# A graph network in three edge stages: a new order of work in the head, in layer 1 and in the attention stage

## The chip, the cores and the metric

The kernel runs on one core of a Trainium2 chip. A core has a matrix engine (PE; its weight loads have a row of their own, PEld), a vector engine (DVE), a scalar engine (ACT), a general-purpose engine (POOL), which here issues the gathers, and SP, which issues plain transfers. Engines run side by side and wait for one another through semaphores. The metric is the device time of one execution in microseconds (us); lower is better.

## The reference, cut to what matters

The graph has N = 12500 nodes with D = 128 features and E = 400000 edges, sorted by target node. Two relational layers with R = 10 relations are followed by one attention layer with 4 heads of 32 features (GAT).

```python
def _rgcn_layer(x, src, dst, edge_type, w_rel, root, bias):
    seg = dst * NUM_REL + edge_type
    xs = x[src]
    sums = segment_sum(xs, seg); cnt = segment_sum(ones, seg)
    mean = (sums / maximum(cnt, 1)).reshape(N, NUM_REL, -1)
    return einsum('nrd,rdo->no', mean, w_rel) + x @ root + bias

# first block
edge_type = argmax(edge_attr_42[:, 16:26])
h = relu(layernorm(x))
x = x + _rgcn_layer(relu(_rgcn_layer(h, ..., w_rel1, root1, b1)), ..., w_rel2, root2, b2)
# second block (GAT)
h = relu(layernorm(x))
xl, xr = h @ W_l, h @ W_r                    # 4 heads x 32
score = einsum(leaky_relu(xr[dst] + xl[src], 0.2), att)
ex = exp(score - segment_max(score, dst)[dst])
out = segment_sum(ex / segment_sum(ex)[dst] * xl[src])
x = x + out + bias
```

## The kernel before, in words

The edges are cut into G = 125 groups of 128 x 25: a partition holds 25 edges that follow one another, and a group covers few enough target nodes that a 128-wide window of nodes holds them. The relational layers are turned round: a table of `h @ w_rel` for every node and relation is computed first, and each edge then gathers its row of 128 floats. So the program has four stages.

1. **Head** (`first_table`, to about 283 us): node tiles of 128 are normalised (`stats`, `norm`), transposed on PE (`turn`), put through a ReLU on ACT (`relu`) and multiplied with the ten matrices `wall`; the table goes to memory in 640 KB stores. A quad is four tiles and has one load of `x`. SP issues all 26 loads of `x` at the start, with the two edge lists `dst_i` and `src_i` as whole transfers between them. `analysis` is a generator whose steps run one per tile, from tile LEAD on.
2. **Layer 1** (`layer1`, to about 4890 us): the edge sums of the first layer, and from each finished 128-node window the table of the second layer.
3. **Layer 2** (`layer2`, to about 9320 us): the edge sums of the second layer, and the products `xl`, `xr` for GAT.
4. **GAT** (the code from L860, to 14040 us).

Stages 2 to 4 are loops with one turn per group. The order of the instructions within a turn is written by hand (`tc.manual_schedule()`): each engine runs its instructions in the order of the code, across groups at different depths. POOL issues in each turn 25 indirect gathers of one row per partition (L496 in the layers, L479 in GAT), as far ahead as there are free buffers: in layer 1 six half groups `xs`, in GAT five groups `xs`. A gather into a buffer waits for its last reader.

*A turn t of layer 1*, in this order: the gathers of group t and the loads; `node(t-2)`, which takes the PE sums `ps` of its group (carry add at L697), finds the carry `last` and makes `hT` with a ReLU on ACT (L706); `prepare(t+4)`, which finds relations and counts and sends their ends through PE (px, L624) to ACT (`ro`, L627); for group t-1 the `one_hots`, 24 `products` on ACT (L528, the second half of the edges, 13 + 12 edges to the halves and two products an edge) and `half_sums` on DVE (L516 and L519, the wide sum of the first half); `table(t-3)`, three matmuls (L714) with three copies on ACT (L716), one add on DVE (L718) and two stores by SP; `inflow(t+2)`, which begins with a copy of the carry `tr` on ACT (L650); `weights(t+1)`; `keep(t+5)` (ACT, L598); last the second half's reduction (L534) and `sums` (PE, L553) with the root matmul (L770). `ke` and `px` have one buffer each, `pt` and `ps` two.

*A turn t of GAT*: the gathers of t; two `z` copies by ACT (L931), each of up to 7 edges' target rows, from the PSUM tile `xn` (made by `prepare` in the turn before: PE multiplies one-hots `st` with the node rows `xr`, for the first and the last target of each half); `score(0)` to `score(3)`, each of them one copy_predicated (L937), an add with the gathered rows (L939), the leaky ReLU with `att` (L941) and a reduction (L943) on DVE; between them `inflow` and `end` and `add_up` of group t-3; then `maxima(t-1)` (two transposes on PE, L957, and the ACT copy `ro`, L960), `prepare(t)`, and ACT's copy `su` of the sums (`take`). `add_up` ends with `sums`: five pairs of a scaled block `xw` (DVE L1002, and a column copy by ACT, L1005) and a one-hot block `s` (DVE L1007), each pair feeding five matmuls (L1011). `xw` and `s` come from the pool `go`, four buffers each.

Of the kernel before, what the change touches and what calls it, by code (L numbers as in the profile page):

```python
# [18 lines left out]
P = 128  # L19
# [7 lines left out]
def kernel(  # L27
# [299 lines left out]
    def first_table():  # L327

        Q = 4
        LEAD = 12  # L330
        full = N // P
# [3 lines left out]
        tiles = [(q, k) for q, ts in enumerate(quads) for k in range(len(ts))]  # L335
        with tc.tile_pool(name="vw", bufs=1) as wp, tc.tile_pool(name="vx", bufs=1) as xp, \
                tc.tile_pool(name="vh", bufs=4) as hp, tc.tile_pool(name="vt", bufs=4) as tp, \
# [3 lines left out]
            wall = wp.tile([P, R * D], F32, name="wall")  # L341
            b2b = bcast_row(wp, b2, "b2b")
            dst_i = ap.tile([P, G, J], I32, name="dst_i")
            xs = []
            for q, ts in enumerate(quads):
                n = len(ts)
                r = starts[ts[0]]
                xq = xp.tile([P, Q, D], F32, name=f"xq{q}")
                nc.sync.dma_start(xq[:, :n, :], x[r:r + n * P, :].rearrange("(k p) d -> p k d", p=P))
                xs.append(xq)  # L350
                if q == 0:
                    nc.scalar.dma_start(wall.rearrange("d (r o) -> d r o", r=R), w_rel1.rearrange("r d o -> d r o"))
                if q == min(3, len(quads) - 1):
                    nc.sync.dma_start(dst_i, dstv)
                if q == min(6, len(quads) - 1):
                    nc.sync.dma_start(src_i, srcv)
            nc.sync.dma_start(hT_d[:, NP - P:], zero[:, :P])
            nc.sync.dma_start(xb_d[NP - P:, :], zero[:, :D])
            tv = t1_d.rearrange("(n r) d -> n (r d)", r=R)
# [47 lines left out]
            for i in range(3):  # L407
                norm(i)
            for i in range(2):
                turn(i)  # L410
                relu(i)
            look = analysis(ap, pp, dst_i)
            for i, (q, k) in enumerate(tiles):
                hT = hTs[q][:, k, :]
                ts = tp.tile([P, R * D], F32, name="ts")
# [26 lines left out]
                if k == n - 1:  # L442
                    r = starts[quads[q][0]]
                    xb = xp.tile([P, Q, D], F32, name=f"xb{q % 2}")
                    nc.vector.tensor_add(xb[:, :n, :], xs[q][:, :n, :], b2b[:, None, :].to_broadcast([P, n, D]))
                    nc.sync.dma_start(xb_d[r:r + n * P, :].rearrange("(k p) d -> p k d", p=P), xb[:, :n, :])
                    nc.sync.dma_start(hT_d[:, r:r + n * P], hTs.pop(q)[:, :n, :].rearrange("d k p -> d (k p)"))
            for _ in look:
                pass


    def sorted_edges():
# [4 lines left out]
        with tc.tile_pool(name="sd", bufs=1, space=DRAM) as sd, tc.tile_pool(name="sk", bufs=1) as sk:  # L457
# [29 lines left out]
            with tc.tile_pool(name="mid", bufs=1) as mid:  # L487
# [68 lines left out]
                def layer1():  # L556
                    with tc.tile_pool(name="fk", bufs=1) as kp, tc.tile_pool(name="fx", bufs=6) as xp, \
# [87 lines left out]

                        def inflow(g, rs, ps, before):

                            tr = wp.tile([R, P + 1], F32, name="tr")
                            if g:
                                nc.scalar.copy(tr[:, 0:1], before[:, P:])  # L650
                            else:
                                nc.vector.memset(tr[:, 0:1], 0.0)
                            nc.vector.tensor_tensor_scan(tr[:, 1:], ps[g][:, 0, :], rs[g][2][:, 0, :], tr[:, 0:1],
                                                         op0=OP.mult, op1=OP.add)
# [13 lines left out]
                            nc.scalar.copy(io, pc)  # L668
                            return io, tr

# [38 lines left out]
                        def table(g, hT, xb, b):  # L709
                            ts = wp.tile([P, (R + 1) * D], F32, name="ts")  # L710
                            for c in range(0, (R + 1) * D, 512):
                                n = min(512, (R + 1) * D - c)
                                pt = p3.tile([P, 512], F32, name="pt")
                                nc.tensor.matmul(pt[:, :n], hT, wall[:, c:c + n], start=True, stop=True)  # L714
                                m = min(n, R * D - c)
                                nc.scalar.copy(ts[:, c:c + m], pt[:, :m])  # L716
                                if m < n:
                                    nc.vector.tensor_add(ts[:, R * D:], pt[:, m:n], xb)  # L718
                            nc.sync.dma_start(t2v[ds(b, P), :], ts[:, :R * D])
                            nc.sync.dma_start(acc2_d[g], ts[:, R * D:])  # L720

# [4 lines left out]
                        with tc.manual_schedule():  # L726
                            for t in range(-4, G + 3):
# [10 lines left out]
                                if 0 <= q < G:  # L738
                                    nodes[q] = load_node(q)
                                q = t - 2  # L740
                                if 0 <= q < G:
                                    hTs[q], last = node(q, pss.pop(q), last)
                                q = t + 4
                                if 0 <= q < G:
                                    rs[q] = prepare(q, ms.pop(q), ke)
                                q = t - 1
                                if 0 <= q < G:
                                    ss = one_hots(sp, q)
                                    y1 = products(yp, by_slot(sp, q, 1), xs[q][1], 1)
                                    rr = [half_sums(yp, sp, by_slot(p2, q, 0), xs[q][0], 0)]  # L750
                                q = t - 3
                                if 0 <= q < G:
                                    table(q, hTs.pop(q), *nodes.pop(q)[1:])
                                q = t + 2
                                if 0 <= q < G:
                                    ios[q], tr = inflow(q, rs, ps, tr)
                                q = t + 1
                                if 0 <= q < G:
                                    weights(q, *rs[q][:2], keep(q), ios.pop(q))
                                    rs.pop(q), ps.pop(q)  # L760
# [3 lines left out]
                                if 0 <= q < G:  # L764
# [6 lines left out]
                                                     skip_group_check=True)  # L771
                                    xs.pop(q)

                def layer2():
# [86 lines left out]
            with tc.tile_pool(name="gk", bufs=1) as kp, tc.tile_pool(name="gx", bufs=5) as xp, \  # L861
                    tc.tile_pool(name="gw", bufs=2) as wp, tc.tile_pool(name="gs", bufs=3) as sp, \
                    tc.tile_pool(name="go", bufs=4) as op, \
                    tc.tile_pool(name="gc", bufs=4) as cp, tc.tile_pool(name="gn", bufs=6) as np_, \
# [5 lines left out]
                iotap = bank[:, :P]  # L870
                exps = [bank[:, k * P:k * P + H * J].rearrange("p (h j) -> p h j", h=H) for k in (1, 2)]
                nc.vector.tensor_copy(iotap, iota)
                att8 = kp.tile([P, D], F32, name="att8")
# [19 lines left out]
                def flat(t):  # L893
                    return t.rearrange("p h j -> p (h j)")
# [101 lines left out]
                def sums(g, xs, sc, po, before):  # L996
                    ex = exps[g % 2]
                    nc.scalar.activation(ex, sc, AF.Exp)
                    ex = ex.rearrange("p h j -> p j h")
                    for j0 in range(0, J, JW):  # L1000
                        xw = op.tile([P, JW, H, AW], F32, name="xw")
                        nc.vector.tensor_mul(  # L1002
                            xw[:, :, :, :C], xs[:, j0:j0 + JW, :D].rearrange("p j (h c) -> p j h c", h=H),
                            ex[:, j0:j0 + JW, :, None].to_broadcast([P, JW, H, C]))
                        nc.scalar.copy(xw[:, :, :, C], ex[:, j0:j0 + JW, :])  # L1005
                        s = op.tile([P, JW, P], F32, name="s")
                        nc.vector.tensor_tensor(s, iotap[:, None, :].to_broadcast([P, JW, P]),  # L1007
                                                dst_b[:, g, j0:j0 + JW, None].to_broadcast([P, JW, P]),
                                                op=OP.is_equal)
                        for j in range(JW):  # L1010
# [31 lines left out]
                with tc.manual_schedule():  # L1042
                    for t in range(G + 1):
# [485 lines left out]
```

## Time and profile before

| what | value |
|---|---|
| runs, median (lowest to highest) | 14032.24 us (14024.25 to 14067.41) |
| profiled execution | 14041.59 us |
| its span on the core | 14039.8 us |
| mean granted PE clock | 0.558 of full |
| DVE busy | 9212.9 us, 66% |
| POOL busy | 9120.0 us, 65% |
| PE and PEld busy | 3446.7 us and 2310.3 us |
| ACT busy | 2298.5 us |
| layer 1, 280 to 4890 us: DVE / POOL / ACT busy | 2838.0 / 2967.4 / 1365.6 us |
| GAT, 9560 to 14040 us: DVE / POOL / ACT busy | 3465.2 / 2829.2 / 689.5 us |

A group's row in the page names its line, engine and operation, the tiles written and read, the count, the busy time with the mean of one instruction in ns, and the engine's idle time just before such instructions with what ended it. "issue" is a wait for nothing that the profile shows, "remote" one for which no releaser was found. A line of the timeline gives start, duration, engine, line, operation, tiles and count, and in brackets the idle time before it with its releaser; an end of a matmul in it is modelled. The gathers' own busy time is the making of their descriptors, and a small issue time between two of them is not counted as busy.

### The profile page before, as it was taken

The numbers are of one execution on the slowest core, as the hardware profiler recorded it, in microseconds if no ns is written. First come the engines' busy times: TensorE is split into PE (matmuls) and PEld (weight loads), VectorE is DVE, ScalarE is ACT, GpSimd is POOL, SyncE is SP. The second block draws the span as 40 slices with busy tenths as digits, with TensorE's granted clock in tenths as the row PEclk, the third lists the DMA queues.
The fourth block names the chain that finished last, engine by engine and source line by source line (L and its number), as shares of the span: only waits on it lengthen the run. The fifth ranks groups of instructions, "written<-read, shape, count | busy, mean of one in ns | idle before, by whom it ended". The sixth has DMA issues, their size and how long they took to land.

```text
span 14039.8 us, 68433 instructions
## 1 busy us (share of the span) xinstructions
PE 3446.7 (25%) x12832; PEld 2310.3 (16%) x12832; DVE 9212.9 (66%) x12638; ACT 2298.5 (16%) x6975; POOL 9120.0 (65%) x9384
## 2 busy tenths in 40 slices
PE   6122222222222211111111111112333333333333
PEld 3011111111111100000000000002222222222223
DVE  7566666666666565555555565656777777777777
ACT  2233223333232200000000000001111111111111
POOL 1666666666666577777777666655666666666664
PEclk8555555555555555555555555555666666666666
DMA  8222222222222211111111111111222222222221
GB/s 274 76 82 85 84 81 86 83 83 86 85 81 86 70 56 54 54 54 54 54 54 54 53 55 54 55 49 50 56 56 57 56 56 57 56 52 56 57 56 40
DMA packets 595938, 964.56 MB, mean 69 GB/s; under 512 B 190432, under 2 KB 397866, under 8 KB 595498
## 3 DMA queue, kind: packets, MB, share of 16 engines
q0 software_dynamic: 300000, 621.40, 16.5%
q1 hardware_dynamic: 280090, 273.82, 6.2%
q10 hardware_dynamic: 15408, 64.89, 1.2%
q14 instruction: 336, 2.75, 0.1%
q8 instruction: 104, 1.70, 0.0%
HBM read 758.60 MB, written 200.85 MB: 68 GB/s over the span
## 4 chain that ended last, share of the span: by engine, by line
issue 28%; DVE 27%; POOL 19%; another core or an unknown queue 12%; PE 6%; ACT 5%; DMA 2%; SPq 0%; DVEq 0%; ACTq 0%; POOLq 0%
POOL xs L496 14%; POOL xs L479 5%; ACT y L528 3%; DVE z L939 2%; DVE lr L941 2%; DVE y L516 2%; PE po L1011 2%; DVE xw L1002 2%; DVE sc L943 2%; DVE r L534 2%; DVE z L937 2%; DVE s L1007 1%; DVE r L519 1%; DMA xs<-xl_d,src_i 1%
## 5 line engine op out<-in xcount | busy, mean ns | idle before, releaser
L496 POOL DMA_INDIRECT xs<-t_d,idx x6250 | 6146.7, 983 | 2821.1 <-issue 1867.4
L479 POOL DMA_INDIRECT xs<-xl_d,src_i x3125 | 2971.4, 951 | 1690.9 <-issue 913.0
L519 DVE TENSOR_REDUCE r<-y 128x256 f32<-128x3072 f32 (+1 forms) x375 | 2102.9, 5608 | 30.5 <-DVE y L516 0.5
L516 DVE TENSOR_TENSOR y<-xs,wk 128x3072 f32<-128x3072 f32 (+1 forms) x375 | 1324.4, 3532 | 368.5 <-DMA xs<-t_d,idx 237.0
L1011 PE MATMUL po<-xw,s 128*128 128x132 f32 x6250 | 1101.5, 346 | 1323.5 <-issue 1030.4
L1011 PEld LDWEIGHTS po<-xw,s 128*128 128x128 f32 x6250 | 1019.5, 252 | 1385.8 <-issue 1054.3
L553 PE MATMUL ps<-r,s 128*128 128x128 f32 x1000 | 305.6, 461 | 3528.0 <-issue 1905.8
L714 PE MATMUL pt<-wall,hT 128*128 128x512 f32 x750 | 640.9, 991 | 1391.0 <-remote 865.0
L807 DVE TENSOR_TENSOR x<-sm,ac 128x128 f32<-128x128 f32 x125 | 36.4, 291 | 1420.0 <-DMA xl_d<-ts 1030.5
L528 ACT ACTIVATE y<-xs,wk 128x128 f32<-128x128 f32 x3000 | 933.6, 488 | 148.4 <-issue 92.2
L937 DVE COPY_PREDICATED z<-mk,xn 128x896 f32<-128x896 int32 x500 | 491.1, 982 | 561.5 <-ACT z L931 284.2
L553 PEld LDWEIGHTS ps<-r,s 128*128 128x128 f32 x1000 | 231.9, 322 | 3654.9 <-issue 1974.7
L1002 DVE TENSOR_TENSOR xw<-xs,bank 128x640 f32<-128x640 f32 x625 | 508.9, 814 | 304.4 <-remote 164.0
L1007 DVE TENSOR_TENSOR s<-bank,dst_b 128x640 f32<-128x640 f32 x625 | 515.4, 825 | 170.0 <-issue 89.9
L931 ACT COPY z<-xn 128x896 f32<-128x896 f32 x500 | 395.0, 812 | 909.7 <-DVE lr L941 689.8
L939 DVE TENSOR_TENSOR z<-xs,z 128x896 f32<-128x896 f32 x500 | 497.8, 996 | 39.3 <-DMA xs<-xl_d,src_i 22.4
L941 DVE SCALAR_TENSOR_TENSOR lr<-z,att 128x896 f32<-128x896 f32 x500 | 495.2, 990 | 17.1
L943 DVE TENSOR_REDUCE sc<-lr 128x28 f32<-128x896 f32 x500 | 493.9, 988 | 17.1
L553 PE MATMUL ps<-s,r 128*128 128x128 f32 x1000 | 305.5, 461 | 806.6 <-issue 433.3
L718 DVE TENSOR_TENSOR ts<-pt,xb 128x128 f32<-128x128 f32 x125 | 35.5, 284 | 697.6 <-ACT tr L650 649.5
L714 PEld LDWEIGHTS pt<-wall,hT 128*128 128x128 f32 x750 | 209.8, 320 | 1701.9 <-remote 942.9
L534 DVE TENSOR_REDUCE r<-y 128x256 f32<-128x3072 f32 x125 | 411.9, 3295 | 0.0
(211 smaller groups left out, 5834.7 us busy)
## 6 DMA issues: line engine op xcount, KB each, us to landing
xs<-t_d,idx POOLq DMA_INDIRECT x6250
t_d<-ts SPq DMA_DIRECT2D x125, 640.0 KB
m<-in_edge_attr_dram SPq DMA_DIRECT2D x125, 525.0 KB
t_d<-ts ACTq DMA_DIRECT2D x98, 640.0 KB
xs<-xl_d,src_i POOLq DMA_INDIRECT x3125
db<-drow_d SPq DMA_DIRECT2D x125, 128.0 KB
xl_d<-ts SPq DMA_DIRECT2D x125, 66.0 KB
at<-hT_d SPq DMA_DIRECT2D x125, 64.0 KB
```

The source lines that it names most:

```text
L479: nc.gpsimd.indirect_dma_start(out=xs[:, j, :], out_offset=None, in_=table, in_offset=bass.IndirectOffsetOnAxis(ap=ids[:, j:j + 1], axis=0))
L496: nc.gpsimd.indirect_dma_start(out=x[:, j, :], out_offset=None, in_=table, in_offset=bass.IndirectOffsetOnAxis(ap=ids[:, j0 + j:j0 + j + 1 ...
L516: nc.vector.tensor_mul(y[:, :, :n, :], xs[:, None, :n, :].to_broadcast([P, 2, n, D]), wk[:, :, :n, None].to_broadcast([P, 2, n, D]))
L519: nc.vector.tensor_reduce(r, y[:, :, :n, :].rearrange("p c j d -> p c d j"), AX.X, OP.add)
L528: nc.scalar.activation(y[:, c, :, j], xs[:, j, :], AF.Copy, scale=wk[:, c, j:j + 1])
L553: nc.tensor.matmul(ps, a, b, start=(k == 0 and c == 0), stop=(k == 1 and c == 1), skip_group_check=True)
L714: nc.tensor.matmul(pt[:, :n], hT, wall[:, c:c + n], start=True, stop=True)
L939: nc.vector.tensor_add(z, xs[:, j0:j0 + n, :D], z)
L941: nc.vector.scalar_tensor_tensor(lr[:, :n, :], z, 0.0, att8[:, None, :].to_broadcast([P, n, D]), op0=OP.max, op1=OP.mult)
L943: nc.vector.tensor_reduce(sc[:, :, j0:j0 + n].rearrange("p h j -> p j h"), lr[:, :n, :].rearrange("p j (h c) -> p j h c", h=H), AX.X, OP.add)
L1002: nc.vector.tensor_mul(xw[:, :, :, :C], xs[:, j0:j0 + JW, :D].rearrange("p j (h c) -> p j h c", h=H), ex[:, j0:j0 + JW, :, None].to_broadc ...
L1011: nc.tensor.matmul(po, s[:, j, :], xw[:, j].rearrange("p h a -> p (h a)"), start=(j0 + j == 0), stop=(j0 + j == J - 1), skip_group_check=True)
```

## The change

It has three parts. Nothing is changed in what is computed, and layer 2 isn't touched.

*Head.* The loads of `x` are issued six quads ahead, from the loop, into eight rotating buffers; the lists come in eight pieces of 32 groups, one a quad. The load of `wall` is first. The first tiles' normalisation follows quad 0's statistics at once, and the row `b2b` and the two zero stores come after it. LEAD goes from 12 to 8. `xb` moves to a pool of four buffers.

*Layer 1.* The copy of the carry (`carried`) and `keep(t+1)` stand right behind `prepare`, ahead of the products; `node(t-2)` stands behind `half_sums`; `inflow` stands ahead of `table`; `table` hands back its last part (the add L718 and the store of `acc2_d`), which runs at the end of the turn.

*GAT.* `prepare(t)` stands between `score(1)` and `end`; its result `xn` is copied by ACT to an SBUF tile `xt` (two buffers), from which `z` is then made; the mask `mk` lies in the PSUM bank beside `exps`; in `sums`, `s` is built ahead of `xw`; the pool `go` has five buffers.

```diff
@@ first_table
-        LEAD = 12
+        LEAD = 8
+        AHEAD = 6
-                nc.sync.dma_start(xq[:, :n, :], x[r:r + n * P, :].rearrange("(k p) d -> p k d", p=P))
-                if q == min(3, len(quads) - 1):
-                    nc.sync.dma_start(dst_i, dstv)
-                if q == min(6, len(quads) - 1):
-                    nc.sync.dma_start(src_i, srcv)
+            def load_x(q):
+                if q < len(quads):
...
+                    xs[q] = xp.tile([P, Q, D], F32, name="xq")
+                    nc.sync.dma_start(xs[q][:, :n, :], x[r:r + n * P, :].rearrange("(k p) d -> p k d", p=P))
+            GC = 32
+            lists = [(a, b, g, min(g + GC, G)) for a, b in ((dst_i, dstv), (src_i, srcv)) for g in range(0, G, GC)]
...
             for i, (q, k) in enumerate(tiles):
+                if k == 0:
+                    load_list()
+                    load_x(q + AHEAD)
@@ layer1
-                        def inflow(g, rs, ps, before):
+                        def carried(g, before):
                             tr = wp.tile([R, P + 1], F32, name="tr")
                             if g:
                                 nc.scalar.copy(tr[:, 0:1], before[:, P:])
...
+                            return tr
+                        def inflow(g, rs, ps, tr):
@@ table
-                                if m < n:
-                                    nc.vector.tensor_add(ts[:, R * D:], pt[:, m:n], xb)
                             nc.sync.dma_start(t2v[ds(b, P), :], ts[:, :R * D])
-                            nc.sync.dma_start(acc2_d[g], ts[:, R * D:])
+                            def add():
+                                nc.vector.tensor_add(ts[:, R * D:], pt[:, m:n], xb)
+                                nc.sync.dma_start(acc2_d[g], ts[:, R * D:])
+                            return add
@@ turn of layer1
-                                    hTs[q], last = node(q, pss.pop(q), last)
                                 q = t + 4
                                     rs[q] = prepare(q, ms.pop(q), ke)
+                                if 0 <= t + 1 < G:
+                                    ke = keep(t + 1)
+                                if 0 <= t + 2 < G:
+                                    tr = carried(t + 2, tr)
                                 q = t - 1
...
                                     rr = [half_sums(yp, sp, by_slot(p2, q, 0), xs[q][0], 0)]
-                                    table(q, hTs.pop(q), *nodes.pop(q)[1:])
+                                    hTs[q], last = node(q, pss.pop(q), last)
...
-                                    ios[q], tr = inflow(q, rs, ps, tr)
+                                    ios[q] = inflow(q, rs, ps, tr)
+                                    add = table(q, hTs.pop(q), *nodes.pop(q)[1:])
...
-                                    weights(q, *rs[q][:2], keep(q), ios.pop(q))
+                                    weights(q, *rs[q][:2], ke, ios.pop(q))
...
+                                if add:
+                                    add()
@@ GAT
-                    tc.tile_pool(name="go", bufs=4) as op, \
+                    tc.tile_pool(name="go", bufs=5) as op, \
+                others = [bank[:, k * P + H * J:k * P + (H + 1) * J] for k in (1, 2)]
@@ prepare of GAT
-                    mk = wp.tile([P, J], F32, name="mk")
+                    mk = others[g % 2]
...
-                    return xn, mk.bitcast(I32), flat(pk)
+                    xt = wp.tile([P, 4, D], F32, name="xt")
+                    nc.scalar.copy(xt, xn)
+                    return xt, mk.bitcast(I32), flat(pk)
@@ sums of GAT: the four lines that make s move ahead of those that make xw
@@ turn of GAT
                         score(1)
+                        if t < G:
+                            xn[t] = prepare(t, xr.pop(t), dbs.pop(t))
                         if q >= 1:
                             end(q - 1)
...
                             sms[a], ros[a] = maxima(xs[a], scs[a], pks[a])
-                        if t < G:
-                            xn[t] = prepare(t, xr.pop(t), dbs.pop(t))
```

More of the change, by code (lines that the diff above doesn't have):

```diff
@@ L335, in first_table @@
         tiles = [(q, k) for q, ts in enumerate(quads) for k in range(len(ts))]
-        with tc.tile_pool(name="vw", bufs=1) as wp, tc.tile_pool(name="vx", bufs=1) as xp, \
+        with tc.tile_pool(name="vw", bufs=1) as wp, tc.tile_pool(name="vx", bufs=AHEAD + 2) as xp, \
                 tc.tile_pool(name="vh", bufs=4) as hp, tc.tile_pool(name="vt", bufs=4) as tp, \
@@ L341, in first_table, with load_list @@
             wall = wp.tile([P, R * D], F32, name="wall")
-            b2b = bcast_row(wp, b2, "b2b")
             dst_i = ap.tile([P, G, J], I32, name="dst_i")
[L344 to L348, printed above, removed]
-                nc.sync.dma_start(xq[:, :n, :], x[r:r + n * P, :].rearrange("(k p) d -> p k d", p=P))
-                xs.append(xq)
-                if q == 0:
-                    nc.scalar.dma_start(wall.rearrange("d (r o) -> d r o", r=R), w_rel1.rearrange("r d o -> d r o"))
-                if q == min(3, len(quads) - 1):
-                    nc.sync.dma_start(dst_i, dstv)
-                if q == min(6, len(quads) - 1):
-                    nc.sync.dma_start(src_i, srcv)
-            nc.sync.dma_start(hT_d[:, NP - P:], zero[:, :P])
-            nc.sync.dma_start(xb_d[NP - P:, :], zero[:, :D])
+            xs = {}
+            def load_x(q):
+                if q < len(quads):
+                    n = len(quads[q])
+                    r = starts[quads[q][0]]
+                    xs[q] = xp.tile([P, Q, D], F32, name="xq")
+                    nc.sync.dma_start(xs[q][:, :n, :], x[r:r + n * P, :].rearrange("(k p) d -> p k d", p=P))
+            GC = 32
+            lists = [(a, b, g, min(g + GC, G)) for a, b in ((dst_i, dstv), (src_i, srcv)) for g in range(0, G, GC)]
+            def load_list():
+                if lists:
+                    a, b, g0, g1 = lists.pop(0)
+                    nc.sync.dma_start(a[:, g0:g1, :], b[:, g0:g1, :])
+            nc.scalar.dma_start(wall.rearrange("d (r o) -> d r o", r=R), w_rel1.rearrange("r d o -> d r o"))
+            for q in range(AHEAD):
+                load_x(q)
             tv = t1_d.rearrange("(n r) d -> n (r d)", r=R)
@@ L406, in first_table @@
                 scales()
[L407 to L411, printed above, removed]
+                if q == 0:
+                    for i in range(3):
+                        norm(i)
+                    for i in range(2):
+                        turn(i)
+                        relu(i)
+            b2b = bcast_row(wp, b2, "b2b")
+            nc.sync.dma_start(hT_d[:, NP - P:], zero[:, :P])
+            nc.sync.dma_start(xb_d[NP - P:, :], zero[:, :D])
             look = analysis(ap, pp, dst_i)
             for i, (q, k) in enumerate(tiles):
+                if k == 0:
+                    load_list()
+                    load_x(q + AHEAD)
                 hT = hTs[q][:, k, :]
@@ L443, in first_table @@
                     r = starts[quads[q][0]]
-                    xb = xp.tile([P, Q, D], F32, name=f"xb{q % 2}")
+                    xb = hp.tile([P, Q, D], F32, name="xb")
                     nc.vector.tensor_add(xb[:, :n, :], xs[q][:, :n, :], b2b[:, None, :].to_broadcast([P, n, D]))
@@ L447, in first_table @@
                     nc.sync.dma_start(hT_d[:, r:r + n * P], hTs.pop(q)[:, :n, :].rearrange("d k p -> d (k p)"))
+            while lists:
+                load_list()
             for _ in look:
@@ L668, in inflow @@
                             nc.scalar.copy(io, pc)
-                            return io, tr
+                            return io
                         def weights(g, rh, rm, ke, io):
@@ L739, in layer1 @@
                                     nodes[q] = load_node(q)
-                                q = t - 2
-                                if 0 <= q < G:
-                                    hTs[q], last = node(q, pss.pop(q), last)
                                 q = t + 4
@@ L750, in layer1 @@
                                     rr = [half_sums(yp, sp, by_slot(p2, q, 0), xs[q][0], 0)]
-                                q = t - 3
+                                q = t - 2
                                 if 0 <= q < G:
-                                    table(q, hTs.pop(q), *nodes.pop(q)[1:])
+                                    hTs[q], last = node(q, pss.pop(q), last)
                                 q = t + 2
                                 if 0 <= q < G:
-                                    ios[q], tr = inflow(q, rs, ps, tr)
+                                    ios[q] = inflow(q, rs, ps, tr)
+                                q = t - 3
+                                add = None
+                                if 0 <= q < G:
+                                    add = table(q, hTs.pop(q), *nodes.pop(q)[1:])
                                 q = t + 1
                                 if 0 <= q < G:
-                                    weights(q, *rs[q][:2], keep(q), ios.pop(q))
+                                    weights(q, *rs[q][:2], ke, ios.pop(q))
                                     rs.pop(q), ps.pop(q)
@@ L1000, in sums @@
                     for j0 in range(0, J, JW):
+                        s = op.tile([P, JW, P], F32, name="s")
+                        nc.vector.tensor_tensor(s, iotap[:, None, :].to_broadcast([P, JW, P]),
+                                                dst_b[:, g, j0:j0 + JW, None].to_broadcast([P, JW, P]),
+                                                op=OP.is_equal)
                         xw = op.tile([P, JW, H, AW], F32, name="xw")
@@ L1005, in sums @@
                         nc.scalar.copy(xw[:, :, :, C], ex[:, j0:j0 + JW, :])
[L1006 to L1009, printed above, removed]
                         for j in range(JW):
```

## The prediction, made before the change was run

> **What bounds the kernel now.** I read the page's groups first, for the engine each stage hangs on, then windows by stage, then the waits and the timeline of single turns.
>
> ```profile
> L496 POOL DMA_INDIRECT xs<-t_d,idx x6250 | 6146.7, 983 | 2821.1 <-issue 1867.4
> L479 POOL DMA_INDIRECT xs<-xl_d,src_i x3125 | 2971.4, 951 | 1690.9 <-issue 913.0
> ...
> L1002 DVE TENSOR_TENSOR xw<-xs,bank 128x640 f32<-128x640 f32 x625 | 508.9, 814 | 304.4 <-remote 164.0
> ...
> L718 DVE TENSOR_TENSOR ts<-pt,xb 128x128 f32<-128x128 f32 x125 | 35.5, 284 | 697.6 <-ACT tr L650 649.5
> ```
>
> Every edge stage issues 25 gathers a turn on POOL. One is 0.945 us and a gap of 0.305 follows, 1.25 in all, so a turn can't be under 31.25. Where POOL never waits, in layer 2 up to 7670 us, a gather takes 1.05 to 1.08 and a turn 35.0, so 31.25 may not last. Layer 1 now takes 73.4 us for two turns (starts of L516: 25.8, then 47.6), GAT 36.36. So POOL waits: about 11.1 us every second turn in layer 1, 5.3 in every GAT turn. What for, GAT's timeline shows (start, duration, instruction, idle before and releaser):
>
> ```profile
> 10518.32 0.82 DVE L1002 TENSOR_TENSOR xw<-xs,bank 128x640 f32<-128x640 f32 x1 [2.14 <-remote]
> ...
> 10519.41 0.94 POOL L479 DMA_INDIRECT xs<-xl_d,src_i  x1 [5.31 <-DVE xw L1002]
> ...
> 10533.21 1.10 DVE L937 COPY_PREDICATED z<-mk,xn 128x896 f32<-128x896 int32 x1 [3.52 <-issue]
> ```
>
> The fifth `xw` takes the buffer of the first (`go` has four) and waits 2.14 us for the first five matmuls. Those ended at 10513.37, but PE's semaphore moved only at 10518.30, 4.2 us after POOL had stopped issuing (10514.1). It is the same everywhere that I followed updates: after some 20 us of unbroken gathers, PE's and ACT's completions come about 0.70 us apart (1.40 for a matmul with its weight load), and the backlog is gone 4.2 to 4.6 us after POOL goes idle. DVE's are prompt. The turn in which POOL's pause was too short shows the price:
>
> ```profile
> 12335.50 0.82 DVE L1002 TENSOR_TENSOR xw<-xs,bank 128x640 f32<-128x640 f32 x1 [2.03 <-PE po L1011]
> ...
> 12336.59 0.95 POOL L479 DMA_INDIRECT xs<-xl_d,src_i  x1 [3.95 <-DVE xw L1002]
> ...
> 12372.46 0.36 ACT L960 COPY ro<-px 4x256 f32<-4x256 f32 x1 [26.63 <-remote]
> ...
> 12374.69 1.10 DVE L937 COPY_PREDICATED z<-mk,xn 128x896 f32<-128x896 int32 x1 [27.82 <-ACT z L931]
> ```
>
> The pause was 3.95 us, PE then got on at 1.40 a matmul, `ro`'s copy waited 26.63 for the transposes behind the burst and kept the next `z` copies behind it on ACT. It cleared at 12372.2, 4.6 us after POOL ran out of free buffers (12367.6). That turn took 60.6 us, the next 34.1. So the wait for `xw`'s buffer, which looks like waste, is what pauses POOL long enough in each turn. Layer 1 has the same thing, every second turn:
>
> ```profile
> 2509.18 1.65 PE L714 MATMUL pt<-wall,hT 128*128 128x384 f32 x2 [15.88 <-remote]
> ...
> 2510.86 0.37 ACT L716 COPY ts<-pt 128x256 f32<-128x256 f32 x1 [9.54 <-issue]
> ...
> 2511.96 0.29 DVE L718 TENSOR_TENSOR ts<-pt,xb 128x128 f32<-128x128 f32 x1 [10.84 <-ACT tr L650]
> ```
>
> The 24 products on ACT ended at 2499.14, the last one's semaphore moved at 2507.73; the table's third piece waits for its copies (PE 15.88 us), its own copy is at 2510.86 after 9.54 us of idle ACT, and DVE stands at L718 for 10.84.
>
> **The change, part by part.**
>
> *Head.* The 26 loads of `x` and the two lists leave the front of SP's queue, where the third `x` load sat from 8.97 to 25.0 us and left PE idle for 12.24 us at 47.38. The stage is 283 us, PE 90% busy in it, so what is late next is PE and the table stores. LEAD, pools and eight list loads, one a quad behind the quad's `x` load on SP, lie beside PE. Bounds 0 and −25; I take −10, the PE stall less its refill.
>
> *Layer 1.* `tr`'s early copy (0.18 us, L650) and `keep` now stand before the 24 products (7.2 us) on ACT, so they no longer wait for the table's copies. L718 (0.29) and its store go to the turn's end, by which time the copies are done: the 10.84 us go. `node` behind the wide sum (3.5 + 5.6 us) gives PE's sums that much longer: L697's wait of up to 8.4 goes. Instructions are the same in number, and SP sees one store of 64 KB later. Now late: the products' own completion at the turn's last reduction, and `inflow`, whose px transposes and `io` copy queue behind a delayed PE and ACT. DVE is busy 625 of 1000 us, some 23 of a turn; with continuous gathers ACT's about 34 completions at 1.40 need 48. So turns stay mixed: I estimate three in 106 us (32, 24 to 25 and a cleared one of about 50), 35.4 a turn for 36.7, over 118 turns −150. Bounds: −230 (POOL at the 35.0 it holds in layer 2, and the stage's ends too) and +150 (one longer clearing in six turns).
>
> *GAT, what it takes off DVE.* Of a free turn, as the one after the long one, 34.1 us: between `maxima` and the next `z` DVE has 4.2 us, ending in `z`'s wait for `xn` (3.52), since `prepare` stands there. With `prepare` in mid turn `xn` is early; in the gap remain PE's two transposes, `ro`, `su` and two `z` copies on ACT, 2.6. `prepare`'s comparisons, 0.77, which ran in the gap, now stand on DVE's path. The copy to `xt` is one more ACT operation a turn (L931's 0.81 is the nearest row, for 896 elements; 512 here, so about 0.5), beside DVE in mid turn; if it isn't hidden, all 0.5 falls on `score(2)`. `mk` in PSUM and `xt` in SBUF change an operand each of L937 (982 ns): no row shows that pair; L1002 with one operand in each memory takes 814 ns for 640 elements, and L939 996 for 896, so ±0.1 us for each of four pieces, and nothing is taken. `s` ahead of `xw` removes the five waits of L1007 on ACT's column copy (0.26 each), of which it gives back most at the first pair. 34.1 − 4.2 + 2.6 + 0.77 − 0.4 = 32.9 us.
>
> *GAT, what it takes from POOL.* With five buffers the fifth `xw` waits for no matmul of its own turn, only for the previous turn's. POOL's pause becomes 32.9 − 31.3 = 1.6 us, where 4.2 were needed and 3.95 did not do. A turn has 25 matmuls in the burst, 4 for `xn` and 4 transposes, each with its weight load: 33 × 1.40 = 46 us of completions if POOL never pauses. That doesn't fit in 32.9, so the backlog grows until `ro` is late, ACT holds `z` back, DVE stops, and POOL runs out of buffers. Worked out from a cleared turn: its last `xw` at X; the next at X + 32.9; POOL fills the freed buffer until X + 64.3; the backlog clears 6.5 later (4.6 after 25 gathers, 7.5 to 8 after 50; I take between), X + 70.8; `ro` to `z` is 2.3, and `z` to the last `xw` 21.3: X + 94.4. Two turns in 94.4 are 47.2 each; the long turn and its follower in the trace are 60.6 + 34.1 = 94.7. Over 122 turns (47.2 − 36.36) × 122 = +1320, of which the one long turn was there already, −24.
>
> Two rules of the Trainium skill bear here. "SBUF — State Buffer", section on who interferes with whom, says that only the port pair which VectorE and GpSimd share causes contention, and that PE and ACT wait on nobody. By it matmuls beside gathers complete on time, and GAT falls to 32.9: −420. The rows above (26.63, 15.88) show PE and ACT late beside POOL, and 0.945 us for gathers beside L1002 shows no lost port; I go by the rows, +1296. "Trainium Kernel Development and Optimization", best practices, advises double buffering for overlap; a fifth buffer is its kin, worth the 2.14 us a turn, −260, by the rule. The pause of 3.95 beside the one of 5.31 says it costs.
>
> Sum against the profiled execution: 14041.6 − 10 − 150 + 1320 − 24 = 15,178; the median of the runs lies 9 us lower: 15,170.
>
> **Rivals.**
> 1. *The pause isn't needed (faster).* `ro`'s transposes might get through with 1.6 us of pause, or a slower gather (the 1.40 of layer 2) brings its own rhythm. For it: layer 2 runs unbroken for 80 turns, though with a tenth of the matmuls. Against: 3.95 us didn't clear. GAT at 35.0 to 32.9 saves 165 to 420, with the others 13,700 to 13,450.
> 2. *The lock finds a new place.* DVE waits in each turn for `ro` just long enough to pause POOL by 5 us: GAT 36.4 to 37.5, −0 to +134, with layer 1 13,870 to 14,020. For it: 36.36 is such a balance. Against: `ro` stands behind the whole burst, not behind its first five.
> 3. *Clearing in part.* Long turns are fewer, every third to sixth: a long turn costs about 26 over 33 to 34, so GAT takes 37 to 42 and the time is 14,050 to 14,800.
> 4. *Layer 1 loses its pauses too.* Then its ACT needs 48 us a turn: +11 × 118 = +1300 on top, 16,400.
>
> **How the numbers follow.** The forecast has 0.42 (14,850 to 15,450), rival 1 0.20, rival 2 0.09, rival 3 0.23, rival 4 0.06. The likeliest's own range is 14,850 to 15,450: 45.0 to 49.0 us a turn, layer 1 −230 to +150. All cases from 13,600 to 15,400 leave out about 0.12 below and 0.08 above. A measurement tells 0.3% from no change, 42 us. Faster takes rival 1 and most of rival 2: 0.25; same 0.04; slower 0.71.
>
> **What would show it.** Right: in GAT, starts of a turn's fifth `xw` (L1002) alternate between about 33 and 61 us, `ro` waits over 20 us every second turn, POOL's gaps alternate between under 2 and over 25 us, and the wait of `xw` for matmuls is gone. Layer 1: L718's wait gone, stage 35 to 36 us a turn. Head: `x` never late, the first layer 1 gather 10 us earlier. Wrong: GAT turns under 36.4 with pauses under 3 us would break the rule of the pause; a free GAT turn far from 33 us breaks the sum on DVE.

## The result, and the profile after

The changed kernel takes 15126.01 us (15111.13 to 15145.73, 4 runs) against 14028.24 us (the kernel before, 4 runs): a ratio of 1.0778 (1.0753 to 1.0803), 7.8% slower. The profiled execution spans 15114.8 us. By the first gather of each stage the two traces divide so:

| stage | before, us | after, us | difference |
|---|---|---|---|
| head, to the first gather of layer 1 | 296.2 | 273.4 | −23 |
| layer 1 | 4595.5 | 4481.4 | −114 |
| layer 2, unchanged | 4449.6 | 4449.3 | 0 |
| GAT | 4698.5 | 5910.7 | +1212 |

First a group of the page before, then those of the page after (lines have moved: L494 is GAT's gather, L969 the copy_predicated, L1038 `xw`):

```profile
L937 DVE COPY_PREDICATED z<-mk,xn 128x896 f32<-128x896 int32 x500 | 491.1, 982 | 561.5 <-ACT z L931 284.2
```

```profile
L494 POOL DMA_INDIRECT xs<-xl_d,src_i x3125 | 2949.8, 944 | 2929.5 <-DVE xw L1038 1922.1
...
L969 DVE COPY_PREDICATED z<-bank,xt 128x896 f32<-128x896 int32 x500 | 493.7, 987 | 1888.2 <-ACT z L963 1826.7
...
L1038 DVE TENSOR_TENSOR xw<-xs,bank 128x640 f32<-128x640 f32 x625 | 506.5, 810 | 0.0
```

The busy times are those of before. What moved is idle time: `xw` no longer waits (304.4 before, 0.0), the gathers wait 1239 us longer, and DVE waits 1888.2 us at `z` in place of 561.5. One pair of GAT turns in the timeline after:

```profile
10321.52 0.94 POOL L494 DMA_INDIRECT xs<-xl_d,src_i  x1 [4.38 <-DVE xw L1038]
...
10330.45 0.42 PE L990 MATMUL px<-ident,dn 128*4 128x128 f32 x1
...
10357.22 0.36 ACT L992 COPY ro<-px 4x256 f32<-4x256 f32 x1 [27.24 <-remote]
...
10358.58 1.10 DVE L969 COPY_PREDICATED z<-bank,xt 128x896 f32<-128x896 int32 x1 [28.18 <-ACT z L963]
...
10380.52 0.94 POOL L494 DMA_INDIRECT xs<-xl_d,src_i  x1 [28.11 <-DVE xw L1038]
...
10389.92 0.36 ACT L992 COPY ro<-px 4x256 f32<-4x256 f32 x1 [0.93 <-PE px L990]
...
10391.27 1.10 DVE L969 COPY_PREDICATED z<-bank,xt 128x896 f32<-128x896 int32 x1 [1.86 <-ACT z L963]
...
10415.82 0.94 POOL L494 DMA_INDIRECT xs<-xl_d,src_i  x1 [4.40 <-DVE xw L1038]
```

From 10321.52 to 10380.52 is a long turn, from there to 10415.82 a short one. After a pause of 4.38 us `ro` starts 27 us after PE began the second transpose that it waits for, and DVE stands at `z` for as long; after the pause of 28.11 it is on time. So PE's work was under way long before; what is late is its completion, the report of its end to the engine that waits. This alternates through the stage, 58 short turns (median 35.2) and 56 long ones (59.5).

The kernel before itself took 14,028 to 14,399 us on some occasions (called *late* below) and 12,494 to 12,500 us on others (*prompt*, where no completion was late and POOL never paused within the layers), so each run below is set against the kernel before on its own occasion.

### The profile page after: what moved, and what is told of

Its sections match the earlier page's. It is cut to its first block, busy times and chain, and to the rows that moved or that the text cites. A ratio compares the mean times of both kernels' runs of the same rounds, so it can differ in the third digit from the quotient of the medians.

```text
span 15114.8 us, 69192 instructions
## 1 busy us (share of the span) xinstructions
PE 3499.9 (23%) x12832; PEld 2382.4 (16%) x12832; DVE 9210.5 (61%) x12638; ACT 2406.9 (16%) x7100; POOL 9142.7 (60%) x9384
## 4 chain that ended last, share of the span: by engine, by line
DVE 28%; issue 23%; another core or an unknown queue 20%; POOL 19%; PE 4%; ACT 4%; DMA 2%; DVEq 0%; ACTq 0%; SPq 0%; POOLq 0%
POOL xs L511 18%; DVE r L534 4%; DVE xw L1038 3%; DVE y L531 3%; DVE z L971 3%; DVE lr L973 2%; DVE z L969 2%; DVE sc L975 2%; ACT y L543 1%; PE po L1043 1%; DMA xs<-xl_d,src_i 1%; PE ps L433 1%; PE xn L955 1%; POOL xs L494 1%
## 5 line engine op out<-in xcount | busy, mean ns | idle before, releaser
L494 POOL DMA_INDIRECT xs<-xl_d,src_i x3125 | 2949.8, 944 | 2929.5 <-DVE xw L1038 1922.1
L969 DVE COPY_PREDICATED z<-bank,xt 128x896 f32<-128x896 int32 x500 | 493.7, 987 | 1888.2 <-ACT z L963 1826.7
L1043 PE MATMUL po<-xw,s 128*128 128x132 f32 x6250 | 1233.2, 355 | 1103.3 <-issue 826.5
L1043 PEld LDWEIGHTS po<-xw,s 128*128 128x128 f32 x6250 | 1098.7, 258 | 1216.3 <-issue 905.7
L543 ACT ACTIVATE y<-xs,wk 128x128 f32<-128x128 f32 x3000 | 972.4, 488 | 257.0 <-issue 237.9
L963 ACT COPY z<-xt 128x896 f32<-128x896 f32 x500 | 404.0, 822 | 646.2 <-DVE lr L973 376.4
L1038 DVE TENSOR_TENSOR xw<-xs,bank 128x640 f32<-128x640 f32 x625 | 506.5, 810 | 0.0
L684 PE MATMUL px<-ident,tr 10*128 10x10 f32 x125 | 30.6, 245 | 2045.5 <-DVE tr L672 717.8
L522 DVE SCALAR_TENSOR_TENSOR wk<-dst_f,w 128x12 f32<-128x12 f32 (+1 forms) x1000 | 213.5, 233 | 374.8 <-remote 238.3
```

The lines of the kernel that those rows point to most:

```text
L494: nc.gpsimd.indirect_dma_start(out=xs[:, j, :], out_offset=None, in_=table, in_offset=bass.IndirectOffsetOnAxis(ap=ids[:, j:j + 1], axis=0))
L543: nc.scalar.activation(y[:, c, :, j], xs[:, j, :], AF.Copy, scale=wk[:, c, j:j + 1])
L969: nc.vector.copy_predicated(z, mk[:, j0:j0 + n, None].to_broadcast([P, n, D]), xn[:, 2 * k + 1, None, :].to_broadcast([P, n, D]))
L1038: nc.vector.tensor_mul(xw[:, :, :, :C], xs[:, j0:j0 + JW, :D].rearrange("p j (h c) -> p j h c", h=H), ex[:, j0:j0 + JW, :, None].to_broadc ...
L1043: nc.tensor.matmul(po, s[:, j, :], xw[:, j].rearrange("p h a -> p (h a)"), start=(j0 + j == 0), stop=(j0 + j == J - 1), skip_group_check=True)
```

## The experiments

**Four at once, prompt.** Each changes one thing: g1 puts back four buffers in the changed kernel, g2 gives the kernel before five, g3 joins the new head and layer 1 with the old GAT, g4 adds one POOL instruction a turn.

```diff
g1: changed kernel                     g2: kernel before
-  tc.tile_pool(name="go", bufs=5)     -  tc.tile_pool(name="go", bufs=4)
+  tc.tile_pool(name="go", bufs=4)     +  tc.tile_pool(name="go", bufs=5)
g4: changed kernel, gather of GAT
   xs = pool.tile([P, J, n], F32, name="xs")
+  nc.gpsimd.iota(rest, pattern=[[1, 1400]], base=0, channel_multiplier=0, ...)
   for j in range(J):
```

> The changed kernel with four buffers in go again, nothing else put back. Theory (PE's completions queue up while POOL issues, and only a pause of some 4.2 to 4.6 us per 25 gathers clears them; the fifth buffer took that pause away): the fifth s waits for the first five matmuls, and this holds POOL until they are reported, 31.3 + 4.2 + 1.7 for s and xw = 37.2 us a turn in GAT, no alternation; 13,850 to 14,000 in all. Rival (prepare in mid turn, or the copy to xt, makes the long turns): alternation stays, 15,000 to 15,200. Rival of the buffer's rule (fewer buffers, more waiting): slower than the changed kernel.

> The kernel before with five buffers in go, nothing else of the change. Theory: POOL's pause falls from 5.3 to 34.1 - 31.3 = 2.8 us, turns of about 60 and 34 alternate, 47 us a turn, 15,200 to 15,450. Rival (the new order of GAT is to blame, not the buffer): the 2.14 us of waiting go, GAT 34 to 35 a turn, 13,750 to 13,900.

> Head and layer 1 of the changed kernel, GAT of the kernel before. If the parts add up, as the traces of the two kernels have it (head -23, layer 1 -114): 13,890. If layer 1's gain is given back where the stages meet: 14,000 to 14,030.

> The changed kernel with one more POOL instruction in each GAT turn, ahead of its gathers: an iota of 128x1400 into a tile that nobody reads, about 5.1 us. Nothing waits for PE because of it. Theory (it is the pause in the gathers that counts, not whom POOL waits for): 31.3 + 5.1 + 0.3 = 36.7 us a turn, no long turns, 13,850 to 13,950, so added work makes the kernel some 1,200 us faster. Rival (the long turns come from a wait in the new order): the short turns get longer, the long ones stay, 15,100 to 15,500.

| run | us | ratio to the kernel before (12,493.92) | GAT turn, mean |
|---|---|---|---|
| g1 | 12,314.03 | 0.9856 (0.984 to 0.9873) | 32.25 |
| g2 | 12,486.84 | 0.9995 (0.9986 to 1.0004) | 33.62 |
| g3 | 12,485.56 | 0.9994 (0.9985 to 1.0003) | 33.68 |
| g4 | 12,319.04 | 0.9861 (0.9845 to 0.9878) | 32.68 |

No expectation was met, since each took late completions for granted. Gathers run at 1.25 us without a pause through both layers (31.4 to 31.6 and 31.25 us a turn, in place of 36 and 35). So layer 1's new order is worth nothing here: in g3 the head is 23 us shorter than in g2, layer 1 some 10 us longer.

**The changed kernel itself, prompt (g5).**

> The changed kernel itself. In the first four experiments POOL never paused in the layers and no turn was late (kernel before 12,494 us where the prediction was measured against 14,028), so what this kernel does there isn't known. Theory: without late completions the fifth buffer costs nothing and GAT is bound by DVE at 32 to 33 us or POOL at 31.25: if the chip is such a one, 12,270 to 12,330, some 1.5% faster than the kernel before. If completions are late on it (kernel before about 14,030), 15,100 to 15,150 as before. Rival (the long turns belong to the new order, on any chip): some 1,000 us slower than the kernel before on either.

12,311.11 us, ratio 0.9848 (0.9832 to 0.9865), as its theory had it: the change that costs 7.8% saves 1.5% here. The waits in GAT, first of g2 (old order), then of g5 (new order), each over 8500 to 12200 us, with total, count and longest:

```profile
DVE z L937 <- ACT z L931: 379.8, 108, 3.5
...
POOL xs L479 <- DVE xw L1002: 274.4, 91, 3.3
...
DVE s L1007 <- ACT xw L1005: 141.3, 542, 0.3
```

```profile
DVE z L969 <- ACT z L963: 210.7, 113, 1.9
...
POOL xs L494 <- DVE xw L1038: 131.6, 74, 2.1
DVE s L1034 <- ACT xw L1041: 124.4, 452, 0.6
```

The wait at `z` falls from 3.5 to 1.9 us a turn, as `prepare` is out of its way; that is the gain of the new order. A DVE turn falls by 1.4 us (34.1 to 32.7, medians of g2 and g5), and the stage by 164. `s` ahead of `xw` gives little back: `s` still waits about 0.27 us for the column copy of the `xw` before it, in four of a turn's five blocks (452 waits in 113 turns, 542 in 108 before), and all waits at the two lines fall only from 1.70 to 1.49 us a turn. The fifth buffer is worth nothing that can be told from noise here: 12,487 against 12,494 in the kernel before (g2), and g1 and g5 are 3 us apart.

**Four buffers and early `z` copies, late (g6).** The first two `z` copies of the next turn go ahead of `maxima` on ACT.

```diff
-  zs = [first_xr(xn[a][0], p) for p in PARTS[:2]]
+  zs = early
...
   score(3)
+  if t < G:
+      early = [first_xr(xn[t][0], p) for p in PARTS[:2]]
   if work:
       pks[a] = xn.pop(a)[2]
```

> The changed kernel with four buffers in go, and the first two z copies of the next GAT turn issued on ACT ahead of maxima's copies instead of behind them. Where nothing is late (kernel before about 12,495): DVE's wait at the first z, 1.9 us a turn there, goes, DVE's turn is 30.8 and POOL's 25 gathers at 1.25 us bound GAT: 31.3 to 31.6 us a turn for 32.7, 12,150 to 12,200. If instead the two copies only push ro and the late ACT work onto DVE: 12,300 or more. Where completions are late (kernel before about 14,030), theory: the fifth s holds POOL until the first matmuls are reported, 37.2 us a turn, 13,850 to 14,000.

13,987.67 us against 14,047.06, ratio 0.9955 (0.9938 to 0.9971). Now completions were late, and the turn is the forecast 37.24 us, with no long one after the start. The timeline:

```profile
10972.92 0.82 DVE L1034 TENSOR_TENSOR s<-bank,dst_b 128x640 f32<-128x640 f32 x1 [6.64 <-remote]
...
10974.75 0.95 POOL L494 DMA_INDIRECT xs<-xl_d,src_i  x1 [6.33 <-DVE xw L1038]
```

The fifth `s` waits 6.64 us for its buffer, and that wait pauses POOL for 6.33. DVE stands longer in this one place than the kernel before did (2.14), and the turn is still 9.6 us shorter than the changed kernel's. Two things differ from the changed kernel here, though, the buffer and the early copies. `ro` waits only 0.9 us in it, after a pause that the buffer of the fifth `s` makes and not the early copies; but four buffers alone (g1) and the early copies with five were not run on a late occasion, so how much each takes off the turn stays open.

**The buffer alone, the rest and a spacing, late (g7 to g9).** g7 and g8 are the kernels of g4 and g2; g9 has an iota of 128x1 ahead of every gather.

> The kernel of the run g4 once more (the changed kernel, one iota of about 5.1 us on POOL ahead of each GAT turn's gathers), for a chip on which completions are late. There (kernel before about 14,040), theory: the pause in the gathers is what clears them, 36.7 to 37 us a turn, 13,850 to 13,980, so added work takes over 1,100 us off. Rival (clearing needs a wait for PE itself, as in g6): long turns stay, 15,100 to 15,400. Elsewhere 12,319 again.

> The kernel of the run g2 once more (the kernel before with five buffers in go and nothing else). Where completions are late, theory: POOL's pause is 34.1 - 31.3 = 2.8 us, long and short turns alternate, 47 us a turn, 15,250 to 15,450. Rival (the new order of GAT makes the long turns, not the buffer): GAT 34 to 36, 13,750 to 14,000. Elsewhere 12,487 again.

> The changed kernel with a tiny POOL instruction (an iota of 128x1, 0.12 us and its issue) ahead of every single GAT gather: the period of a gather goes from 1.25 to about 1.43 us and no long pause is added. Where completions are late: if it is the sum of POOL's idle time that counts (25 x 0.18 = 4.5 us a turn, as much as the pause that cleared), GAT 36 us a turn without alternation, 13,780 to 13,900. If only an unbroken pause clears: the long turns stay, 15,100 to 15,600. Elsewhere: 25 x 1.43 = 35.8 a turn in place of 32.2, 12,700 to 12,760.

| run | us | ratio to the kernel before (14,071.82) | GAT turn, mean |
|---|---|---|---|
| g7 | 14,640.37 | 1.0404 (1.0355 to 1.0454) | 42.52 |
| g8 | 15,303.60 | 1.0876 (1.0844 to 1.0907) | 46.99 |
| g9 | 15,152.77 | 1.0769 (1.0737 to 1.0800) | 46.84 |

g8 came out as forecast and settles which part does the harm: one digit in the kernel before, and its GAT turn goes from 36.55 to 46.99 (means; the first is from the trace before the change). Its timeline shows the same pair as after, with a pause of 3.21 us before the long turn:

```profile
10438.24 0.95 POOL L479 DMA_INDIRECT xs<-xl_d,src_i  x1 [28.92 <-DVE xw L1002]
...
10448.28 0.36 ACT L960 COPY ro<-px 4x256 f32<-4x256 f32 x1 [0.86 <-PE px L958]
...
10472.48 0.94 POOL L479 DMA_INDIRECT xs<-xl_d,src_i  x1 [3.21 <-DVE xw L1002]
...
10509.10 0.36 ACT L960 COPY ro<-px 4x256 f32<-4x256 f32 x1 [27.44 <-remote]
```

g7 came out between its two theories. Its iota takes 1.32 us, not the 5.1 I had worked out, so most pauses between gathers are 1.3 + 3.4 = 4.7 us, and they clear in part: the first `z` after one waits some 8 us and not 28, but `xt` then waits another 9. g9 came out where long turns had been expected, but tests nothing: the little iotas run within the gap between gathers, whose period is 1.28 us and not 1.43.

**The rest at its right size, and a short burst, late (g10, g11).** g10 has four such iotas a turn; g11 issues one of five matmuls in `sums` (`for j in range(0, 1)`).

> The changed kernel with four iotas of 128x1400 on POOL ahead of each GAT turn's gathers; one of them took 1.32 us in g7, not the 5.1 that was worked out there, so this is 5.3 us without a gather. Where completions are late: if time without gathers clears them, 31.3 + 5.3 and up to 1 us more = 36.6 to 37.6 a turn without long turns, 13,870 to 14,000. If POOL has to be idle, not only without gathers, turns stay uneven at 42 us or more, 14,600 to 15,200. Elsewhere 31.3 + 5.4 = 36.7 a turn for 32.2, 12,830 to 12,870.

> The changed kernel with one matmul of each five in GAT's sums; the other 20 of 25 a turn are left out, so GAT's sums are not the reference's. Vector and scalar work and gathers are the same. Where completions are late, theory (1.40 us for each matmul with its load): 13 a turn need 18 us, which fits in a turn of 33; no long turns, GAT 33 to 35 a turn, 13,420 to 13,700. Rival (ACT's completions alone, about 17 a turn, or any PE wait at all, hold the turn up): above 42 us a turn, 14,500 to 15,100. Elsewhere 12,260 to 12,311: POOL and DVE bound GAT either way.

g10 takes 13,840.76 us, ratio 0.9645 (0.9503 to 0.9786) to a kernel before that was at 14,398.56 (14,248.55 to 14,404.38) beside it. That is 29 us under the expected range; its GAT turn, 36.65 us, is in it and never long:

```profile
11030.32 5.41 POOL L494 IOTA rest<- 128x1400 f32 x4
...
11035.89 0.96 POOL L497 DMA_INDIRECT xs<-xl_d,src_i  x1 [0.15 <-issue]
```

Some 5.6 us without a gather clear the completions, though POOL is busy and no block of `s` or `xw` waits longer than 0.7 us (10500 to 12500 us). So on a late occasion it is the time without gathers that counts, not an idle POOL, and 5.4 us of added work take 10 us off a turn (the changed kernel's 46.84 is from another late occasion).

g11 leaves out 20 of a turn's 25 matmuls. Its two runs (14,145.15 and 15,034.89) lie too far apart for a verdict on the time, so only the trace of the first is read. It has turns of 39 us on average, between the two theories. With 13 matmuls a turn left `ro` still waits up to 11.6 us and `xt` up to 12.1 (10500 to 12500 us), but a shorter pause is enough: in this trace every pause from 3.3 us on clears, and none under 3.1 does. So fewer matmuls make the lateness smaller.

**The early `z` copies, prompt (g12).**

> The kernel of the run g6 once more (the changed kernel, four buffers in go, the first two z copies of a turn issued early). Where nothing is late (kernel before about 12,495): DVE's wait of 1.9 us at the first z goes, GAT is bound by POOL at 31.3 to 31.6 us a turn, 12,150 to 12,220; rival: the early copies hold up ro and sm, 12,300 or more. Where completions are late: 37.2 us a turn in GAT and 13,950 to 14,000 again.

12,134.86 us against 12,497.80, ratio 0.9711 (0.9695 to 0.9727). That is 15 us under the expected range. GAT runs at 31.29 us a turn, POOL's own rate. This kernel is the fastest of the three on both kinds of occasion: by 2.9% against the kernel before where completions are prompt, by 0.45% where they are late (13,988 against 14,047; the changed kernel 15,126 against 14,028).

## Why the prediction was right

The mechanism that carried the forecast is right: the fifth buffer takes away the wait that paused POOL, and long and short turns alternate. Some of its terms were wrong without harm, and what it says holds for late occasions alone, of which its own trace was one; nothing in it foresaw the other kind, where the same change saves 1.5%.

- **GAT, long and short turns.** Two turns were put at 94.4 us and took 94.3 (median of all pairs after, 94.4 in g8). That they come from the fifth buffer is shown by g8, which has it alone; g6, with four buffers and the early copies, has none and runs at the forecast 37.2. The sum was 84 us too high (+1296 against +1212). About half of it is that two short turns sometimes follow one another (58 short to 56 long, 46.84 a turn and not 47.2). The other half is a count: 122 turns were taken, but the first five turns take some 31 us each and the sixth 76 to 77 in both traces, so 118 remain.
- **The pause.** It was put at 1.6 us and is 1.9 to 4.5, since in the turn before a clearing the blocks of `s` and `xw` are up to 2.8 us apart, not 1.8 (`s` waits up to 1.24 there). This was the mis-sized term, and that it did no harm was luck: the true pause is too short as well. The 4.2 to 4.6 us that I took for enough are too few: up to 4.4 clears nothing (after, g7, g8); from 4.4 to 4.9 the outcome varies (nothing in the trace after up to 4.47, in part in most turns of g7, fully in single turns such as one of 4.49 in the kernel before); 5.05 (g7), 5.1 to 5.5 (kernel before), 5.6 (g10) and 6.3 (g6) clear.
- **DVE's free turn**, 32.9, is 32.7 in g5. Of its terms the one for `s` ahead of `xw` (−0.4) was twice too large: it is 0.2.
- **33 completions at 1.40 us.** This counts the matmuls of the code, but the profile has two records to most of them, and 1.40 us is the step from one record to the next (two lines of the long turn of the kernel before, then a group of its page, 50 records a turn):

```profile
12349.05 0.37 PE L925 MATMUL xn<-xr,st 128*128 128x128 f32 x1 [1.08 <-issue]
12350.45 0.37 PE L925 MATMUL xn<-xr,st 128*128 128x128 f32 x1 [1.03 <-issue]
...
L1011 PE MATMUL po<-xw,s 128*128 128x132 f32 x6250 | 1101.5, 346 | 1323.5 <-issue 1030.4
```

  A turn has 64 records (50 of the burst, 8 of `xn`, 6 others), by that step 90 us and not 46. The argument asked only for more than 32.9. g11, put at 18 us, has 24 records or 34 us, which no longer fits its turn of 33, so its late turns don't speak against the step. This is an estimate; no run tests the step itself.
- **Layer 1**, −150, was −114. L718's stall went (697.6 us in the page before, 51.4 at the same addition after), and in its place, as the prediction had it, the turn's last reduction waits for the products (the group before, then after):

```profile
L534 DVE TENSOR_REDUCE r<-y 128x256 f32<-128x3072 f32 x125 | 411.9, 3295 | 0.0
...
L549 DVE TENSOR_REDUCE r<-y 128x256 f32<-128x3072 f32 x125 | 416.6, 3333 | 626.1 <-remote 506.1
```

  The mean turn after is 35.5 us, as put; the mis-sized term is the 36.7 before, which was that of one pair and is 36.3 over the stage. The pattern behind the 35.4 (32, 24 to 25, about 50) isn't in the trace, where turns run from 23 to 46, so that the mean was met was luck. Which of the layer's moves did it wasn't tested. **Head**, −10, was −23, at the far end of its bounds.
- **The skill's rule.** "SBUF — State Buffer" (section on who interferes with whom) would have PE and ACT wait on nobody, which made −420 in GAT. In the prompt runs the trace agrees: gathers without a pause in the layers, `ro` 0.93 us after its transposes in g5. In the late ones, by which the prediction was measured, 27.24 us speak against what was drawn from it. The page is about SBUF's ports, and no run shows that a port is what holds the completions back. The rival of 13,450 to 13,700, the pause isn't needed, had the right sign for the prompt comparisons, though not its size: there the kernel before has no pause of 5.3 us to save either (a GAT turn of 33.68 in g3), and the change is worth 189 us.

## What to carry to other kernels

A wait that a profile shows can be holding something else in check: before taking it away, see what the engine behind it does in the time it will win, and look for a turn in the trace where the wait happened to be short. The gain of an order (here 1.4 us a turn at `z`) and the loss of a buffer came in one change and were told apart only by giving each its own run. Compare with runs beside it, since the time of the same kernel can differ by 12% or more between occasions and a change can have the opposite sign on each.

## What was not expected of the hardware

The same kernel takes 12,494 to 12,500 us on some occasions and 14,028 to 14,399 on others. Where it is slower a gather in an unbroken run takes 1.05 to 1.08 us in place of 0.945 (layer 2: 35.0 to 31.25 us a turn), and PE's and ACT's completions are late beside gathers. The chip's number doesn't decide: g5 and g12 were prompt and g7 to g9 late on chips of the same number. The granted PE clock doesn't either (0.558 in the trace before, 0.559 to 0.565 in the kernel's prompt runs), nor do slower transfers of the gathers: their packets fill 16.6% of 15,287 us in g8 and 20.7% of 12,490 us in g2, much the same time. There is one further sign: the traces of the late occasions hold fewer semaphore updates than there were instructions that make them (DVE: under 4,800 for more than 10,700 in the kernel before and in g6), those of the prompt ones all. So the update times quoted in the prediction come from a record with holes; how long PE, ACT and DVE wait doesn't depend on it, but what a wait is put down to does. Whether the recording itself slows the chip, or something beside the kernel slows both, no run here tells, and it stays open.
